# A selective-scan layer: how VectorE's fills are shared out between two steps, where GpSimd's input rows lie, and when the first copy of z is taken

## The chip, the cores and the metric

The kernel runs on one core of a Trainium2 chip. Its engines work side by side: TensorE (PE) for matmuls, VectorE (DVE), ScalarE (ACT) and GpSimd (POOL) for elementwise work, SyncE (SP) for issuing transfers. The metric is the device time of one execution in microseconds (us): the median of several runs. Lower is better.

## What is computed

The program is a chain of four layers on an image batch of shape (3, 256, 48, 48): a block with attention, two 3x3 convolutions, and a selective-scan (Mamba) layer, each behind a group norm and added to its input. The change touches the last layer alone. Cut to what matters, it is

```python
xz = einsum('blc,dc->bld', layernorm(x), in_proj_w)
x_in, z = split(xz, 2)                       # 512 channels each
u = silu(causal_conv1d(x_in, conv_w))        # 4 taps
dt_raw, B_ssm, C_ssm = split(u @ x_proj_w.T) # 16 states
dt = softplus(dt_raw @ dt_proj_w.T + dt_proj_b)
A = -exp(A_log)

def step(hst, inp):                          # over 2304 tokens
    dt_t, B_t, C_t, u_t = inp
    dA = exp(dt_t[:, :, None] * A)
    hst = hst * dA + dt_t[:, :, None] * B_t[:, None, :] * u_t[:, :, None]
    return hst, einsum('bdn,bn->bd', hst, C_t)

y = (scan(step) + u * D_param) * silu(z)
out = y @ out_proj_w.T
```

## The kernel before, in words

The 3 x 2304 tokens are cut into 18 chunks of 384 tokens (`todo`). The states of a chunk are 512 channels x 16 = 8192 rows, which are 64 tiles of 128 rows. They are worked through in 8 *steps* of 8 rows each: a step is `(at, m, h)`, with the chunk `at`, the block of 128 channels `m` (0 to 3) and the half `h` (0 or 1). So even steps have h = 0, odd ones h = 1, and the two steps of one `m` are a pair. The text counts the steps of a chunk from 0 to 7.

A step has one tile `hs` of the shape (128, 2, 4, 385): two groups `g` of B's rows by four quarters `q` of the channels, and per run one starting state and 384 tokens. There are three such buffers. The tile is filled with dt * u * B, then each of its eight runs is scanned in place, and the result is multiplied by C and summed. In detail, by the lines of the profile:

- `spread` (L1681) reads dt and dt * u from DRAM into the layout of the scan, with transfers that SyncE issues: `dtr` for all four quarters, `dtur` for quarters 2 and 3. `spread_pe` (L1689) puts dt * u for quarters 0 and 1 into the PSUM tile `ps_r` by matmuls. There is one `ps_r`, so a pair's matmuls wait until the pair before has read it.
- `fill` writes a step's products: VectorE quarters 0 and 1 of both groups, from `ps_r` (L1711, 1536 elements a partition), GpSimd quarters 2 and 3, from `dtur` (L1715, 1536 elements). Both read B's rows from SBUF. It stands at the end of the step before.
- `first_states` (L1724) and `last_states` (L1730) copy the one column of states that passes from chunk to chunk, on ScalarE.
- `decay` (L1740) makes exp(dt * A) for one run on ScalarE, in one of three PSUM tiles `ps_da`. It is issued three scans ahead, so that the decay of scan n + 3 waits until scan n has read the same tile.
- `scan` (L1748) runs the recurrence over one run on VectorE. The order of the eight runs is quarters 0, 1 of group 0, then of group 1, then quarters 2, 3 of group 0 and of group 1: the runs that VectorE filled come first.
- `times_c` (L1765) multiplies a step's states by C on GpSimd (3072 elements), behind the GpSimd fill of the next step. `add_states` (L1777, L1782) sums them over the states with matmuls, one step later. `gate` (L1789) multiplies by silu(z) on VectorE, at the end of an odd step, three steps later.

Beside the scan of one chunk the next chunk is prepared and the last one is projected and stored. These stages stand in the tables `plan`, `after` and `gating`: each has a slot 0 to 15 (a step is two slots of four scans), a place in the slot, and the chunk's offset. Places are `MID` (after the second scan and the decay issued with it), `DONE` (after the third), `LATE` (after the fourth), and `PE_` (matmuls, at the middle or the end of a step). A line in the table of this case:

```python
(14, MID, 1, lambda k: take_z(k, 0, 0)),
```

Slot 14 is the first half of step 7, and `take_z` (L1349) copies the first quarter of z from the PSUM bank 0 to SBUF on ScalarE. The bank was written by `project_z` (L1341), and `project_z` of the second quarter needs the same bank next. Ahead of this copy in the same place stands `inverse_root` (L1241, L1242). The two PSUM banks `bank[0]` and `bank[1]` serve all stages in turn, and each stage's matmuls wait until ScalarE or VectorE has read what was there: `taps` (L1264, the convolution) and `take_u` (L1273), `silu` (L1278, with table loads at L1278 and L228), `project_u` (L1284) and `take_dbc` (L1292), `project_dt` (L1310), `softplus` (L1319 to L1321), `take_dt` (L1326, L1327, on VectorE) and `keep_dt` (L1331), `project_y` (L1353, L1355) and `store` (L1365), `less_mean` (L1222), `centre` (L1235, L1237), `square_mean` (L1229), `normalise` (L1246, on VectorE), `tokens` (L1256).

The program's order on TensorE, VectorE, ScalarE and GpSimd is the order in which this code is written: `keep_order` ties each instruction behind the one before it on its engine. Instructions of different engines, and an instruction that needs the result of an earlier one on its own engine, wait on semaphores.

Of the kernel before, what the change touches and what calls it, by code (L numbers as in the profile page):

```python
# [9 lines left out]
F32 = mybir.dt.float32  # L10
I32 = mybir.dt.int32
AF = mybir.ActivationFunctionType
ALU = mybir.AluOpType
# [3 lines left out]
P = 128  # L17
# [8 lines left out]
CH = 384  # L26
# [57 lines left out]
def net(  # L84
# [21 lines left out]
    nc = tc.nc  # L106
# [273 lines left out]
    with ExitStack() as l0:  # L380
# [36 lines left out]
        with ExitStack() as p1:  # L417
# [15 lines left out]
            for b in ORDER:  # L433
# [3 lines left out]
                for ct in range(CT):  # L437
                    for j in range(parts):
                        at = slice(j * N // parts, (j + 1) * N // parts)
# [15 lines left out]
                bb = small.tile([P, 2], F32, name="bb")  # L455
# [592 lines left out]
        chunks = [(b, c) for b in ORDER for c in range(NCH)]  # L1048
# [58 lines left out]
    rooms, w3v, chunks, stored = {}, {}, {}, set()  # L1107

    def room(k, name):
        return rooms[name][k.at % len(rooms[name])]  # L1110
# [228 lines left out]
    def project_z(k, m, j):  # L1339
        for ct in range(CT):  # L1340
            nc.tensor.matmul(  # L1341
                bank[j], w("in", ct * 512 + m * P, P), k.xn[:, ct, DCONV - 1 :],
                start=ct == 0, stop=ct == CT - 1,
            )

    def take_z(k, m, j):
        if m == 0:
            k.sz = room(k, "sz")
        nc.scalar.copy(k.sz[:, m, :], bank[j])  # L1349
# [14 lines left out]
    def store(k, mo):  # L1364
# [7 lines left out]
    MID, DONE, LATE, PE_ = range(4)  # L1372
# [39 lines left out]

    gating = [
        (13, PE_, 1, lambda k: project_z(k, 0, 0)),
        (14, MID, 1, lambda k: take_z(k, 0, 0)),
        (14, PE_, 1, lambda k: project_z(k, 1, 0)),
        (15, MID, 1, lambda k: take_z(k, 1, 0)),
        (15, PE_, 1, lambda k: project_z(k, 2, 0)),
# [237 lines left out]
    with ExitStack() as l3:  # L1656
# [5 lines left out]
        scn = l3.enter_context(tc.tile_pool(name="scn", bufs=2, reuse_waits="tile"))  # L1662
# [10 lines left out]
        def spread(k, m):  # L1673

            dtr = scn.tile([P, 4, CH], F32, name="dtr")
            dtur = scn.tile([P, 2, CH], F32, name="dtur")
            for t, src in ((dtr, k.dtd), (dtur, k.dtud)):
                src = src[m & 2][:, m & 1, :]
                for i in range(4):
                    r = slice(32 * i, 32 * i + 32)  # L1680
                    nc.sync.dma_start(t[r], src.rearrange("(q d) n -> d q n", d=32))  # L1681
            return dtr, dtur
# [13 lines left out]
        steps = [(at, m, h) for at in range(len(todo)) for m in range(DI) for h in range(2)]  # L1696
        tiles = {}
# [4 lines left out]
        for t in slots:  # L1702
            nc.vector.memset(t[:, :1], 0.0)

        def fill(s):

            at, m, h = steps[s]
            k = chunks[at]
            hs = tiles[s]
            bb = k.bc[0][:, 2 * h : 2 * h + 2, :].unsqueeze(2).broadcast_to([P, 2, 2, CH])  # L1710
            nc.vector.tensor_tensor(  # L1711
                hs[:, :, 0:2, 1:],
                k.ps[:, :, :CH].unsqueeze(1).broadcast_to([P, 2, 2, CH]), bb, ALU.mult,
            )
            nc.gpsimd.tensor_tensor(  # L1715
                hs[:, :, 2:4, 1:],
                k.rows[m][1].unsqueeze(1).broadcast_to([P, 2, 2, CH]), bb, ALU.mult,
            )

        def first_states(s):  # L1720
            at, m, h = steps[s]
            src = zero if chunks[at].c == 0 else state[m, h]
            hs = tiles[s] = scn.tile([P, 2, 4, CH + 1], F32, name="hs", bufs=3)
            nc.scalar.copy(hs[:, :, :, 0], src.rearrange("p (g q) -> p g q", g=2))  # L1724

        def last_states(s):
            at, m, h = steps[s]
# [64 lines left out]
        last = len(todo) - 1  # L1792
        k = chunks[0]
        k.rows = {0: spread(k, 0)}
        spread_pe(k, 0)
        first_states(0)
        fill(0)
        for n in range(3):
            decay(n)
        for s, (at, m, h) in enumerate(steps):  # L1800
            if m == 0 and h == 1 and at + 2 <= last:
                fetch(at + 2)
            for part in range(8):
                j = 4 * m + 2 * h + part // 4
                scan(s, part)
                decay(8 * s + part + 3)
                if part == 0 and h == 0:
                    c, n = (at, m + 1) if m + 1 < DI else (at + 1, 0)
                    if c <= last:
                        rows = getattr(chunks[c], "rows", {})  # L1810
                        chunks[c].rows = {**rows, n: spread(chunks[c], n)}
                if part == 4 and s + 1 < len(steps):
                    first_states(s + 1)
                if part % 4 == 1:
                    run(at, j, MID)
                if part % 4 == 2:
                    run(at, j, DONE)
                if h == 1 and part == 7 and s >= 3:
                    gate(*steps[s - 3][:2])
                if part % 4 == 3:  # L1820
                    run(at, j, LATE)
                if part == 3:
                    run(at, j, PE_)
            if s + 1 < len(steps):
                fill(s + 1)
# [10 lines left out]
        k = chunks[last]  # L1836
# [37 lines left out]
def net_kernel(tc, *args):  # L1874

    with tc.tile_pool(name="flag", bufs=1) as pool:
        flag = pool.tile([1, 1], I32, name="flag")
        net(tc, *args, flag, False)
        bad = tc.nc.values_load(flag[:1, :1])
        with tc.If(bad > 0):  # L1880
            net(tc, *args, None, True)
# [77 lines left out]
```

## Time and profile before

| | |
|---|---|
| median of 5 runs | 3459.01 us (3453.64 to 3464.20) |
| the profiled execution | 3455.04 us, span 3453.7 us |
| scan layer within the span | first fill at 2020 us, last scan ends at 3432 us, end at 3454 us |
| one chunk of the scan layer (chunk 10) | 2811.93 to 2890.77 us |
| one scan (L1748) | 0.94 us, 0.85 us from start to start |
| VectorE fill (L1711) | 1.74 us |
| GpSimd fill (L1715), product with C (L1765) | 3.45 us, 6.19 us |
| one decay (L1740) | 0.58 us |
| granted TensorE clock, mean of the span | 0.944 |

The span reaches from the first to the last instruction of the profiled execution; its time as the runs measure it is 1.3 us longer. A row of the timeline gives start, duration, engine, line, operation, tile written and tiles read, and in brackets how long the engine was idle before and who ended that. A row of a group adds the count, the busy time, the mean duration in ns, and the idle time before. A row of a stretch gives for PE, PE's weight loads, DVE, ACT and POOL the busy time and the count, then the granted clock, the share of the DMA engines and GB/s. Rows of waits give the waiting engine and line, who was waited for, the total, the times and the longest.

### The profile page before, as it was taken

To read this page: it belongs to the slowest core of one execution; us is meant where nothing else is said; L and a number is where in the kernel's file an instruction comes from. 1 tells how busy PE (TensorE), PEld (TensorE's weight loads), DVE (VectorE), ACT (ScalarE), POOL (GpSimd) and SP (SyncE) were. 2 spreads that over 40 slices of the span, in tenths; PEclk is the share of its full clock that TensorE was granted. 3 is DMA by queue.
4 is the path that set the end of the run, shared out by engine and by line. 5 is a ranking of instruction groups with operands and counts; after the bars stand their busy time and mean duration, and the time that the engine had idled before them with its cause. 6 is when DMAs were issued, how large, how long until landed. Compare 5 with 4: busy or idle time off the path is not lost.

```text
span 3453.7 us, 51943 instructions
## 1 busy us (share of the span) xinstructions
PE 3121.8 (90%) x20170; PEld 1500.1 (43%) x20170; DVE 2939.8 (85%) x3234; ACT 2351.6 (68%) x3508; POOL 1430.5 (41%) x385
## 2 busy tenths in 40 slices
PE   7999999999999999879999988888888888888885
PEld 4334343443433335457777743333344433333331
DVE  4798899859899994589965379999999999999997
ACT  3788888758888884422224457777777777777774
POOL 0000000000000001110000059999999999999997
PEclk9999999999999999999999989889999999988997
DMA  4000000010000003756301134444444444544441
GB/s 187 5 10 8 8 10 8 8 42 7 9 6 8 10 8 112 248 187 215 133 29 60 52 91 115 109 106 114 120 102 114 103 111 110 120 113 110 113 111 43
DMA packets 167603, 273.95 MB, mean 79 GB/s; under 512 B 30049, under 2 KB 134561, under 8 KB 165426
## 3 DMA queue, kind: packets, MB, share of 16 engines
q1 hardware_dynamic: 154114, 250.48, 26.9%
q10 hardware_dynamic: 13232, 20.06, 1.8%
q8 instruction: 160, 2.62, 0.3%
q14 instruction: 97, 0.79, 0.1%
HBM read 223.12 MB, written 47.10 MB: 78 GB/s over the span
## 4 chain that ended last, share of the span: by engine, by line
PE 53%; DVE 33%; ACT 8%; DMA 3%; issue 2%; POOL 0%; SPq 0%; DVEq 0%; ACTq 0%; POOLq 0%
DVE hs L1748 21%; PE ps_s L637 16%; PE acc L650 14%; PE ps_c L1513 8%; DVE hs L1711 4%; PE ps_g L1222 2%; ACT ps_da L1740 2%; DVE u L295 2%; PE ps_y L461 2%; PE ps_m L664 1%; PE ps_s L1030 1%; PE ps_m L710 1%; ACT L1278 1%; ACT L228 1%; PE acc L528 1%
## 5 line engine op out<-in xcount | busy, mean ns | idle before, releaser
L1748 DVE TENSOR_TENSOR_SCAN hs<-ps_da,hs 128x385 f32<-128x385 f32 x1152 | 1005.5, 938 | 54.3 <-ACT ps_da L1740 35.5
L641 ACT ACTIVATE pt<-ps_s 128x1024 f32<-128x1024 f32 x972 | 942.3, 1022 | 154.8 <-PE ps_s L637 142.4
L856 DVE TENSOR_TENSOR part<-part,pt 128x2048 f32<-128x2048 f32 x396 | 906.6, 2289 | 41.3 <-ACT pt L641 18.5
L1740 ACT ACTIVATE ps_da<-dtr,u 128x384 f32<-128x384 f32 x1152 | 655.9, 582 | 270.7 <-DVE hs L1748 247.9
L163 POOL TENSOR_TENSOR rstd<-ve,mhalf 128x2 f32<-128x2 f32 (+1 forms) x26 | 16.3, 629 | 1475.1 <-DVE ve L161 1475.1
L637 PE MATMUL ps_s<-q,kt 32*128 32x512 f32 (+1 forms) x4320 | 576.7, 592 | 0.1
L650 PE MATMUL acc<-pt,vt 128*32 128x512 f32 (+1 forms) x4320 | 521.1, 561 | 0.2
L1765 POOL TENSOR_TENSOR hc<-hs,x 128x3072 f32<-128x3072 f32 x72 | 445.9, 6193 | 21.1 <-DVE hs L1748 19.2
L1513 PE MATMUL ps_c<-vt,u 128*128 128x288 f32 x1728 | 433.6, 412 | 20.9 <-DVE u L262 20.9
L1765 POOL TENSOR_TENSOR hc<-hs,bc 128x3072 f32<-128x3072 f32 x71 | 438.9, 6181 | 17.3 <-DVE hs L1748 16.2
L1264 PE MATMUL ps_g<-u 128*128 128x384 f32 x1152 | 387.7, 492 | 8.2 <-ACT sz L1349 3.5
L1513 PEld LDWEIGHTS ps_c<-vt,u 128*128 128x128 f32 x1728 | 331.9, 193 | 117.2 <-issue 19.2
L1264 PEld LDWEIGHTS ps_g<-u 128*128 128x128 f32 x1152 | 214.6, 190 | 180.3 <-ACT ps_da L1740 18.7
L637 PEld LDWEIGHTS ps_s<-q,kt 32*128 32x128 f32 x4320 | 195.6, 183 | 198.8 <-issue 120.0
L1782 PE MATMUL ps_y<-hc,u 128*32 128x384 f32 x2304 | 245.6, 549 | 13.2 <-POOL hc L1765 13.2
L1715 POOL TENSOR_TENSOR hs<-dtur,x 128x1536 f32<-128x1536 f32 x72 | 248.1, 3446 | 6.6 <-DMA dtur<-dtud 6.6
L1715 POOL TENSOR_TENSOR hs<-dtur,bc 128x1536 f32<-128x1536 f32 x72 | 249.5, 3465 | 0.0
L650 PEld LDWEIGHTS acc<-pt,vt 128*32 128x32 f32 x4320 | 94.7, 108 | 353.1 <-issue 326.5
L1310 PE MATMUL ps_g<-wconv,u 17*128 17x384 f32 x144 | 79.2, 684 | 82.8 <-ACT x L1331 82.8
L1782 PEld LDWEIGHTS ps_y<-hc,u 128*32 128x32 f32 x2304 | 64.5, 117 | 172.1 <-issue 153.1
L321 POOL MEMSET xpad<- 128x212 f32 x12 | 5.6, 469 | 314.2 <-ACT xpad L1564 235.6
L1222 PE MATMUL ps_g<-wconv,u 128*128 128x384 f32 x144 | 82.9, 747 | 52.0 <-ACT x L1331 52.0
(246 smaller groups left out, 3615.6 us busy)
## 6 DMA issues: line engine op xcount, KB each, us to landing
wconv<-in_we SPq DMA_DIRECT2D x144, 384.0 KB, 4.3
dtr<-dtd SPq DMA_DIRECT2D x288, 192.0 KB, 3.9
dtur<-dtud SPq DMA_DIRECT2D x288, 96.0 KB, 4.2
wconv<-xd SPq DMA_DIRECT2D x36, 384.0 KB, 4.3
x<-bcd SPq DMA_DIRECT2D x72, 192.0 KB, 6.1
dtd<-x SPq DMA_DIRECT2D x36, 384.0 KB, 2.8
bc<-bcd SPq DMA_DIRECT2D x72, 192.0 KB, 6.0
yc<-ycat ACTq DMA_DIRECT2D x18, 576.0 KB, 4.8
```

The source lines that it names most:

```text
L637: nc.tensor.matmul(s[:, j, cols], kt[r, mt * P : (mt + 1) * P], q[r, :n], start=True, stop=True,)
L641: nc.scalar.activation(p[:, h0 : h0 + 2, :], s, AF.Exp)
L650: nc.tensor.matmul(acc[h * HD : (h + 1) * HD, :n], vt[:, mt, g * P + h * HD : g * P + (h + 1) * HD], p[:, h, cols], start=mt == 0, stop=mt ...
L856: ): nc.vector.tensor_tensor(part, first, p, ALU.add)
L1222: nc.tensor.matmul(bank[to], w3v["less"][:, int(to != ct), :], k.xg[:, ct, :], start=ct == 0, stop=ct == CT - 1,)
L1264: nc.tensor.matmul(bank[m % 2], w3v["wtap"][:, tap, ct, m * P : (m + 1) * P], k.xn[:, ct, tap : tap + CH], start=tap == 0 and ct == 0, sto ...
L1513: nc.tensor.matmul(pc[:, :HN], u[:, i, dy, ct, m * P : (m + 1) * P], vt[:, i, ct, dy * TW : dy * TW + HN], start=ct == 0 and dy == 0, stop ...
L1715: nc.gpsimd.tensor_tensor(hs[:, :, 2:4, 1:], k.rows[m][1].unsqueeze(1).broadcast_to([P, 2, 2, CH]), bb, ALU.mult,)
L1740: nc.scalar.activation(slots[n % 3][:, 1 : CH + 1], chunks[at].rows[m][0][:, q, :], AF.Exp, scale=amat[:, col : col + 1],)
L1748: nc.vector.tensor_tensor_scan(b, slots[(8 * s + part) % 3][:, : CH + 1], b, 0.0, ALU.mult, ALU.add)
L1765: nc.gpsimd.tensor_tensor(hc, tiles[s][:, :, :, 1:], cb.broadcast_to([P, 2, 4, CH]), ALU.mult)
L1782: nc.tensor.matmul(k.y_ps[32 * q : 32 * q + 32, :CH], fold, hc[:, g, q, :], start=False, stop=h == 1 and g == 1,)
```

## The change

Three things change.

- VectorE's fill of a pair is cut differently. Before, an even and an odd step's four runs each (two groups of two quarters) were filled ahead of the step. Now six runs are filled ahead of the even step: its own four, and the two of group 0 of the odd step. The two that remain, of group 1, are filled ahead of the odd step. The tile of the odd step is therefore taken one step earlier. GpSimd's fill stays as it is.
- `dtur` gets rows of 400 elements instead of 384, of which elements 8 to 391 are used: the rows start 32 bytes behind the start of the tile, and the tile of two rows grows by 128 bytes, as do the places of the tiles behind it.
- `take_z` of the first quarter moves from `MID` to `DONE` in slot 14, one scan and one decay later.

```diff
-        (14, MID, 1, lambda k: take_z(k, 0, 0)),
+        (14, DONE, 1, lambda k: take_z(k, 0, 0)),
...
-            dtur = scn.tile([P, 2, CH], F32, name="dtur")
+            dtur = scn.tile([P, 2, 16 + CH], F32, name="dtur")[:, :, 8 : 8 + CH]
...
+        def states(s):
+
+            if s not in tiles:
+                tiles[s] = scn.tile([P, 2, 4, CH + 1], F32, name="hs", bufs=3)
+            return tiles[s]
+
+        def b_rows(s, lo, hi):
+            at, m, h = steps[s]
+            rows = chunks[at].bc[0][:, 2 * h + lo : 2 * h + hi, :]
+            return rows.unsqueeze(2).broadcast_to([P, hi - lo, 2, CH])
+
+        def fill_upper(s, lo, hi):
+
+            k = chunks[steps[s][0]]
+            nc.vector.tensor_tensor(
+                states(s)[:, lo:hi, 0:2, 1:],
+                k.ps[:, :, :CH].unsqueeze(1).broadcast_to([P, hi - lo, 2, CH]),
+                b_rows(s, lo, hi), ALU.mult,
+            )
+
         def fill(s):
 
             at, m, h = steps[s]
-            k = chunks[at]
-            hs = tiles[s]
-            bb = k.bc[0][:, 2 * h : 2 * h + 2, :].unsqueeze(2).broadcast_to([P, 2, 2, CH])
-            nc.vector.tensor_tensor(
-                hs[:, :, 0:2, 1:],
-                k.ps[:, :, :CH].unsqueeze(1).broadcast_to([P, 2, 2, CH]), bb, ALU.mult,
-            )
+            if h == 0:
+                fill_upper(s, 0, 2)
+                fill_upper(s + 1, 0, 1)
+            else:
+                fill_upper(s, 1, 2)
             nc.gpsimd.tensor_tensor(
-                hs[:, :, 2:4, 1:],
-                k.rows[m][1].unsqueeze(1).broadcast_to([P, 2, 2, CH]), bb, ALU.mult,
+                states(s)[:, :, 2:4, 1:],
+                chunks[at].rows[m][1].unsqueeze(1).broadcast_to([P, 2, 2, CH]),
+                b_rows(s, 0, 2), ALU.mult,
             )
 
         def first_states(s):
             at, m, h = steps[s]
             src = zero if chunks[at].c == 0 else state[m, h]
-            hs = tiles[s] = scn.tile([P, 2, 4, CH + 1], F32, name="hs", bufs=3)
-            nc.scalar.copy(hs[:, :, :, 0], src.rearrange("p (g q) -> p g q", g=2))
+            nc.scalar.copy(states(s)[:, :, :, 0], src.rearrange("p (g q) -> p g q", g=2))
```

## The prediction

> **What bounds the kernel now.** The change lives in the scan layer, the last 1430 us, so the page's shares over the whole span say little. I read the stage first, over one chunk in steady state (chunk 10, 2812 to 2891 us; a chunk is 8 steps of 8 scans). The columns are the busy time of each engine:
>
> ```profile
> 2812.00:2891.00 79.00, 67.32 (x282) 31.14 (x281) 75.79 (x86) 61.67 (x121) 76.57 (x18) 0.89 0.46 111
> ```
>
> VectorE (third) and GpSimd (fifth) are both full to 96%, and TensorE (first) to 85%. Who waits for whom decides, so next come VectorE's waits from 2040 to 3430 us, and GpSimd's groups:
>
> ```profile
> DVE hs L1748 <- ACT ps_da L1740: 34.9, 52, 1.5
> DVE hs L1748 <- DVE hs L1711: 0.5, 1, 0.5
> DVE ps_g L1326 <- ACT x L1321: 0.2, 1, 0.2
> ...
> L1765 POOL TENSOR_TENSOR hc<-hs,x 128x3072 f32<-128x3072 f32 x72 | 445.9, 6193 | 21.1 <-DVE hs L1748 19.2 <-DVE x L1789 1.7 <-POOL hs L1715 0.3
> L1715 POOL TENSOR_TENSOR hs<-dtur,bc 128x1536 f32<-128x1536 f32 x72 | 249.5, 3465 | 0.0
> L1715 POOL TENSOR_TENSOR hs<-dtur,x 128x1536 f32<-128x1536 f32 x72 | 248.1, 3446 | 6.6 <-DMA dtur<-dtud 6.6
> L1040 POOL TENSOR_TENSOR x<-x,xc 128x768 f32<-128x768 f32 x18 | 34.5, 1917 | 109.3 <-ACT x L1035 91.2 <-DMA wconv<-in_we 18.0
> ```
>
> VectorE never waits for GpSimd here, only for ScalarE's decays; GpSimd waits for VectorE. So VectorE carries the stage, and GpSimd follows close behind. The timeline of VectorE in chunk 10 (start, length, line, idle before) shows where the waits stand and how the fills sit between the scans:
>
> ```profile
> 2811.85 0.53 DVE L1789 TENSOR_TENSOR sz<-ps_y,sz 128x384 f32<-128x384 f32 x1
> 2812.30 1.75 DVE L1711 TENSOR_TENSOR hs<-ps_r,x 128x1536 f32<-128x1536 f32 x1
> 2814.15 6.91 DVE L1748 TENSOR_TENSOR_SCAN hs<-ps_da,hs 128x385 f32<-128x385 f32 x8
> 2820.97 1.73 DVE L1711 TENSOR_TENSOR hs<-ps_r,x 128x1536 f32<-128x1536 f32 x1
> 2822.81 6.91 DVE L1748 TENSOR_TENSOR_SCAN hs<-ps_da,hs 128x385 f32<-128x385 f32 x8
> ...
> 2835.17 4.36 DVE L1748 TENSOR_TENSOR_SCAN hs<-ps_da,hs 128x385 f32<-128x385 f32 x5 [0.58 <-ACT ps_da L1740]
> ...
> 2853.64 4.36 DVE L1748 TENSOR_TENSOR_SCAN hs<-ps_da,hs 128x385 f32<-128x385 f32 x5 [0.57 <-ACT ps_da L1740]
> ...
> 2887.25 0.96 DVE L1748 TENSOR_TENSOR_SCAN hs<-ps_da,hs 128x385 f32<-128x385 f32 x1 [1.10 <-ACT ps_da L1740]
> 2888.12 0.93 DVE L1246 TENSOR_TENSOR wconv<-wconv,ps_g 128x768 f32<-128x768 f32 x1
> 2888.97 1.80 DVE L1748 TENSOR_TENSOR_SCAN hs<-ps_da,hs 128x385 f32<-128x385 f32 x2
> ```
>
> The waits stand in three places: at the fourth scan of steps 2 and 4, behind a SiLU and its two table loads, and at the sixth of step 7, behind the inverse root and the first copy of z. Last, TensorE, which no VectorE wait names, and which is the point of this forecast:
>
> ```profile
> 2817.04 10.59 PE L1264 MATMUL ps_g<-u 128*128 128x384 f32 x32 [0.42 <-ACT x L1349]
> 2827.56 1.50 PE L1782 MATMUL ps_y<-hc,u 128*32 128x384 f32 x16
> 2828.99 0.92 PE L1689 MATMUL ps_r<-x,u 32*128 32x384 f32 x4
> ...
> 2847.28 0.91 PE L1689 MATMUL ps_r<-x,u 32*128 32x384 f32 x4
> ```
>
> From 2817.04 to 2848.19 it runs with no idle. It starts on ScalarE's copy of z (L1349), which is queued behind a decay that waits for the second scan of step 0. Its two L1689 rows write the ps_r that the fills of steps 2 and 4 read: they end at 2829.91 and 2848.19, and those fills start at 2830.08 and 2848.56. The slack is 0.17 and 0.37 us.
>
> **The change, part by part.**
>
> *The fills on VectorE.* A pair of steps has fills of 1536 and 1536 elements; now 1536 and 768, then 768. Dependent work starts 1.85 us after the start of a full fill (2812.30 to 2814.15), 1.84 in odd steps. Independent work starts 0.08 before its predecessor ends (2811.85 against 2811.93), so a 768 behind the full fill starts after 1.67. The nearest row of 768 elements is L1246: the next instruction starts 0.85 after it. I take this, since it also has one operand in PSUM and one in SBUF. The first scan of an even step needs the full fill alone, and of an odd step neither, so neither waits for the 768 to drain. Even: 1.67 + 0.85 - 1.85 = **+0.67**. Odd: 0.85 - 1.84 = **-0.99**. A line through L1789 (384 elements, next start 0.45 later) and the full fill (1.67) gives 0.86 as well. Bounds: 0.83 (half of 1.67) and 0.85 + 0.19 = 1.04, if the even scan waits for the 768 as a scan waits for its fill now (0.10 of gap, 0.08 of lost overlap).
>
> [...]
>
> *The wait that is added.* The 768 fill ahead of an even step writes the odd step's states, in the buffer that L1765 reads two steps before. It is queued ahead of the even step's scans, so if L1765 is late all of them are. In chunk 10 that L1765 ends 3.3 us or more before its place (for step 4: 2840.74 + 6.22 = 2846.96 against 2850.2), so it costs nothing while GpSimd trails by no more than 3 us beyond today.
>
> *The walk through chunk 10* (shift of each step's end against before; a wait that goes is worth its idle plus 0.11, as step 2 is 9.81 long and step 0, without one, 9.12):
> - Step 0: +0.67. The copy of z sits behind the second scan, so TensorE's run moves by +0.67 as well.
> - Step 1: -0.99, leaving -0.32.
> - Fill of step 2: VectorE could start it 0.32 early, but ps_r now ends at 2829.91 + 0.67; with 0.05 for the hand-over it starts at 2830.63, +0.55. This is a new wait of about 0.87.
> - Step 2: +0.55 + 0.67 - 0.69 (the wait behind the SiLU is covered now) = +0.53.
> - Step 3: -0.99 in VectorE's own work, but its last scan waits for a decay behind the store's copy, which waits for TensorE's projection of the same run (+0.67): the step ends at +0.36.
> - Fill of step 4: 2848.19 + 0.67 + 0.05 = 2848.91, +0.35; step 4 ends at +0.35 + 0.67 - 0.68 = +0.34.
> - Step 5: -0.99 would bring the softplus product (L1326) to 2.49 after the step's start, but ScalarE's softplus ends 3.16 after it; L1326 moves from 3.48 to 3.20: -0.28, leaving +0.06.
> - Step 6: +0.67, nothing to cover it: +0.73.
> - Step 7: ScalarE's chain (centre, TensorE's mean of squares, inverse root) is fixed to the end of step 6, so the -0.99 is lost to it.
>
> *The copy of z a part later* helps here: the sixth scan's decay no longer stands behind the copy (0.48, and 0.23 waiting for TensorE), and the scan starts 6.55 instead of 7.21 after step 7's start: -0.66, leaving **+0.07 a chunk**. What is late next is the copy itself, by one decay: the projection queued behind it on TensorE starts after other matmuls anyway. Bounds: 0 (the wait only moves to the next decay) and -0.71 (copy and wait both gone).
>
> *GpSimd's rows 32 bytes off.* GpSimd has 76.6 of 79 us of work and VectorE does not wait for it, so a faster fill buys nothing in the steady state. Bounds by its rows per element: 3.10 us (rate of L1765, 2.02 ns) and 3.83 (rate of L1040, 2.50 ns), against 3.45 now. The two L1715 rows read different buffers of B and differ by 0.02; that is nearest, so I take no change. The padding leaves the four DMAs' count and pieces alone, and no VectorE wait names them.
>
> *Ends.* In the first chunk TensorE has 5 us of slack at both fills, so about -2 us; in the last, which prepares no next chunk, GpSimd trails by up to 4.5 us, so -0.4 at most.
>
> **Sum:** 16 x 0.07 - 2 - 0.4 = -1.3 us on the profiled execution's 3455.0 us (span 3453.7), that is 3453.7. This run lies 4.0 below the median of 3459.0, so on the median: **3458 us**.
>
> **The rivals.**
> - *Faster: TensorE's run is not the limit* (it starts earlier, or has idle that the trace hides). Then the steps add to 0.67 - 0.99 - 0.02 - 0.99 - 0.02 - 0.28 + 0.67 - 0.66 = -1.62 a chunk: 16 x 1.62 + 2 = -28, 3431 us. For it: VectorE's own work does shrink, by 0.32 a pair. Against: 31 us without an idle mark. A half-way case, with only some of the 0.67 passed on, gives 3438 to 3450.
> - *Slower: the even scan waits for the second fill.* At 1.04 for a 768 fill, steps 0, 4 and 6 each cost 0.19 more: 0.57 x 17 = +10, 3468 us. It decides from about 1.01 on, where the total passes 7 us. Against: the scan needs only the first fill.
> - *Slower: GpSimd's fill slows down.* A chunk lasts 78.3 to 78.9 us in this trace, against 76.5 of GpSimd's work: 0.23 to 0.30 a fill to spare. At 3.83 (+0.38) it is short by 0.08 to 0.15, x 8 x 17 = +11 to +20: about 3473 us. It decides from about 3.75 on. For it: GpSimd is nearly full. Against: the two rows 0.02 apart.
> - *The change does nothing:* the offset alone may be that, and it is inside the forecast.
>
> [...]
>
> **How the numbers follow.** About 0.2% (7 us) is what a measurement of this kernel can tell from no change. Forecast (3452 to 3464 of its own): 0.52. TensorE not the limit: 0.13, half-way 0.10. Second fill waited for: 0.12. GpSimd slower: 0.10. Something slower that I don't see: 0.03. So faster 0.23, same 0.52, slower 0.25. The range 3438 to 3474 leaves out the full first rival and tails of the others.
>
> **What would show it.** In the profile after: fills of 1.75 and 0.93 us; scans directly behind the odd one; no ScalarE wait at the fourth scan of steps 2 and 4; a smaller one at the sixth of step 7; and a new one, VectorE's fill waiting for TensorE's L1689, about 0.9 us in each step 2. If that last is missing and TensorE has idle between its two L1689 rows, I am wrong on the fast side; a GpSimd fill of over 3.75 us, or a gap between the second fill and the scan, puts me wrong on the slow side.

## The result, and the profile after

The changed kernel takes 3454.24 us (median of 25 runs, 3449.55 to 3463.25), the kernel before, run beside it, 3457.09 us (median of 47 runs). The ratio is 0.9993, 95% interval [0.9988, 0.9999]: within the 0.2% that a measurement of this kernel can tell from no change, as forecast, and just below 1.

The same views as before. First VectorE's waits from 2040 to 3430 us in the changed kernel (engine and line that wait, who was waited for, total us, times, longest):

```profile
DVE hs L1766 <- ACT ps_da L1758: 27.1, 37, 0.9
DVE ps_g L1326 <- ACT x L1321: 11.3, 17, 1.2
DVE hs L1719 <- PE ps_r L1689: 4.3, 16, 0.3
DVE x L1807 <- PE ps_y L1800: 3.4, 8, 0.5
DVE sz L1807 <- PE ps_y L1800: 3.2, 8, 0.4
DVE hs L1766 <- POOL hs L1733: 1.6, 2, 0.9
DVE hs L1719 <- POOL hc L1783: 0.5, 1, 0.5
```

The scans (now L1766) wait 27.1 us for decays instead of 34.9. New are the softplus wait (L1326), 11.3 instead of 0.2 us, and two waits on TensorE in step 2: the gate (L1807), 6.6 us in all, and the fill (L1719), 4.3 us. The three waits for GpSimd, 2.1 us together, all stand in the last chunk. Next, the timeline of VectorE in chunk 10 of the changed kernel: steps 0 to 2, the last scan of step 3, the middle of step 5, and the sixth scan of step 7.

```profile
2812.04 0.53 DVE L1807 TENSOR_TENSOR sz<-ps_y,sz 128x384 f32<-128x384 f32 x1
2812.49 2.61 DVE L1719 TENSOR_TENSOR hs<-ps_r,x 128x1536 f32<-128x1536 f32 x2
2815.02 6.89 DVE L1766 TENSOR_TENSOR_SCAN hs<-ps_da,hs 128x385 f32<-128x385 f32 x8
2821.84 0.93 DVE L1719 TENSOR_TENSOR hs<-ps_r,x 128x768 f32<-128x768 f32 x1
2822.69 6.89 DVE L1766 TENSOR_TENSOR_SCAN hs<-ps_da,hs 128x385 f32<-128x385 f32 x8
2829.98 0.56 DVE L1807 TENSOR_TENSOR sz<-ps_y,sz 128x384 f32<-128x384 f32 x1 [0.40 <-PE ps_y L1800]
2830.80 2.62 DVE L1719 TENSOR_TENSOR hs<-ps_r,x 128x1536 f32<-128x1536 f32 x2 [0.27 <-PE ps_r L1689]
...
2847.81 0.96 DVE L1766 TENSOR_TENSOR_SCAN hs<-ps_da,hs 128x385 f32<-128x385 f32 x1 [0.76 <-ACT ps_da L1758]
...
2861.77 0.57 DVE L1326 SCALAR_TENSOR_TENSOR ps_g<-ps_g,x 128x384 f32<-128x384 f32 x1 [0.63 <-ACT x L1321]
...
2887.03 0.96 DVE L1766 TENSOR_TENSOR_SCAN hs<-ps_da,hs 128x385 f32<-128x385 f32 x1 [0.82 <-ACT ps_da L1758]
```

Two fills ahead of an even step take 2.53 us from the start of the first to the start of the scan (2812.49 to 2815.02), where one took 1.85; the fill of 768 ahead of an odd step takes 0.85 (2821.84 to 2822.69). So an even step is 0.68 longer and an odd one 0.99 shorter in VectorE's own work. The fourth scan of steps 2 and 4 no longer waits. TensorE's run in the same chunk:

```profile
2817.89 10.59 PE L1264 MATMUL ps_g<-u 128*128 128x384 f32 x32 [0.37 <-ACT x L1349]
2828.41 1.50 PE L1800 MATMUL ps_y<-hc,u 128*32 128x384 f32 x16
2829.84 0.91 PE L1689 MATMUL ps_r<-x,u 32*128 32x384 f32 x4
...
2848.13 0.91 PE L1689 MATMUL ps_r<-x,u 32*128 32x384 f32 x4
```

It starts 5.77 us after step 0 does (2812.12), as against 5.11 before, and runs on without a gap; the gate waits for its L1800 (done at 2829.91) and the fill for its L1689 (done at 2830.75). GpSimd's fills are as they were (3452 and 3454 ns, before 3446 and 3465), so its rows 32 bytes off did nothing; one of the two groups:

```profile
L1733 POOL TENSOR_TENSOR hs<-dtur,x 128x1536 f32<-128x1536 f32 x72 | 248.5, 3452 | 6.7 <-DMA dtur<-dtud 6.7
```

The walk through chunk 10, step end by step end, in us after the end of the chunk before:

| | step 0 | 1 | 2 | 3 | 4 | 5 | 6 | 7 |
|---|---|---|---|---|---|---|---|---|
| before | 9.12 | 17.79 | 27.60 | 36.26 | 46.07 | 56.86 | 68.11 | 78.84 |
| after | 9.79 | 17.46 | 28.12 | 36.65 | 46.45 | 56.99 | 68.91 | 78.43 |
| shift measured | +0.67 | -0.33 | +0.52 | +0.39 | +0.38 | +0.13 | +0.80 | -0.41 |
| shift forecast | +0.67 | -0.32 | +0.53 | +0.36 | +0.34 | +0.06 | +0.73 | +0.07 |

Seven of eight fit within 0.07. The eighth doesn't, and it is the one that makes the time. In the kernel before, step 7 has two lengths: its chunks last 78.1 to 78.3 us or 78.7 to 79.1, mixed, and chunk 10 is one of the long ones. Against a short one the changed chunk is 0.10 longer. The experiments turned to what makes this length.

### The profile page after: what moved, and what is told of

Same layout as the page of the kernel before. It is cut to its first block, busy times and chain, and to the rows that moved or that the text cites. A ratio compares the mean times of both kernels' runs of the same rounds, so it can differ in the third digit from the quotient of the medians.

```text
span 3453.7 us, 51999 instructions
## 1 busy us (share of the span) xinstructions
PE 3117.4 (90%) x20170; PEld 1498.2 (43%) x20170; DVE 2936.8 (85%) x3306; ACT 2353.2 (68%) x3508; POOL 1430.6 (41%) x385
## 5 line engine op out<-in xcount | busy, mean ns | idle before, releaser
L1766 DVE TENSOR_TENSOR_SCAN hs<-ps_da,hs 128x385 f32<-128x385 f32 x1152 | 1003.5, 935 | 30.5 <-ACT ps_da L1758 27.1
L1800 PE MATMUL ps_y<-hc,u 128*32 128x384 f32 x2304 | 245.1, 548 | 19.5 <-POOL hc L1783 19.1
L1733 POOL TENSOR_TENSOR hs<-dtur,x 128x1536 f32<-128x1536 f32 x72 | 248.5, 3452 | 6.7 <-DMA dtur<-dtud 6.7
L1733 POOL TENSOR_TENSOR hs<-dtur,bc 128x1536 f32<-128x1536 f32 x72 | 248.7, 3454 | 0.0
L1310 PE MATMUL ps_g<-wconv,u 17*128 17x384 f32 x144 | 79.2, 684 | 85.0 <-ACT x L1331 85.0
L1800 PEld LDWEIGHTS ps_y<-hc,u 128*32 128x32 f32 x2304 | 64.2, 117 | 177.9 <-issue 141.0
L1222 PE MATMUL ps_g<-wconv,u 128*128 128x384 f32 x144 | 80.3, 725 | 62.1 <-ACT x L1331 62.1
```

The source lines that it names most:

```text
L1222: nc.tensor.matmul(bank[to], w3v["less"][:, int(to != ct), :], k.xg[:, ct, :], start=ct == 0, stop=ct == CT - 1,)
L1733: nc.gpsimd.tensor_tensor(states(s)[:, :, 2:4, 1:], chunks[at].rows[m][1].unsqueeze(1).broadcast_to([P, 2, 2, CH]), b_rows(s, 0, 2), ALU.mult,
L1766: nc.vector.tensor_tensor_scan(b, slots[(8 * s + part) % 3][:, : CH + 1], b, 0.0, ALU.mult, ALU.add)
L1800: nc.tensor.matmul(k.y_ps[32 * q : 32 * q + 32, :CH], fold, hc[:, g, q, :], start=False, stop=h == 1 and g == 1,)
```

## The experiments

All ratios are to the kernel before, run beside it on the same chip; lengths of steps and chunks come from one profiled execution each.

### One part at a time

**The new fills alone** (the offset and the place of the copy of z as before):

```diff
-        (14, DONE, 1, lambda k: take_z(k, 0, 0)),
+        (14, MID, 1, lambda k: take_z(k, 0, 0)),
...
-            dtur = scn.tile([P, 2, 16 + CH], F32, name="dtur")[:, :, 8 : 8 + CH]
+            dtur = scn.tile([P, 2, CH], F32, name="dtur")
```

> The new fills alone, with the copy of z and the rows of dt*u as before. Theory (TensorE's run from the copy of z to the ps_r matmuls, and ScalarE's chains, hold the steps, so that VectorE's shorter work buys nothing): step 7 keeps its wait of about 0.9 us at the sixth scan, so a chunk is 0.6 to 0.75 us longer than before, 16 of them +10 to +12, first and last chunk -2.4 together: about +8 us, ratio 1.0015 to 1.003. Rival (the fills alone carry the change, VectorE's own work counts, -0.32 a pair and the waits behind the SiLU gone): 1 us or more less a chunk, ratio 0.995 or below.

3470.86 us, ratio 1.0035 [1.0023, 1.0047]. The fills alone lose, as expected, and more than the 1.0015 to 1.003 forecast. Steps 0 to 6 are those of the changed kernel within 0.01 us; step 7 is 10.71 instead of 9.59 (means over chunks 4 to 15).

**The copy of z later, alone** (on the kernel before):

```diff
-        (14, MID, 1, lambda k: take_z(k, 0, 0)),
+        (14, DONE, 1, lambda k: take_z(k, 0, 0)),
```

> The copy of z a part later alone. Theory: the sixth scan of step 7 starts about 0.66 us earlier in each of 16 chunks, TensorE's run starts up to 0.2 later against step 0 and that fits into the slack of its ps_r matmuls: -9 to -11 us, ratio about 0.997. Rival (the copy's wait only moves to the next decay or to TensorE): ratio 0.999 to 1.001.

3456.19 us, ratio 0.9995 [0.9986, 1.0004]: the gain did not come. The decay of the sixth scan did pass ahead of the copy, but step 7 is 10.44 us long with it and without it (means over chunks 4 to 15). What took the gain is on TensorE. The eight matmuls of L1222 (less_mean), for which step 7's normalisation waits, in chunk 10 of the kernel before and then of this one:

```profile
2876.87 5.05 PE L1222 MATMUL ps_g<-wconv,u 128*128 128x384 f32 x8 [3.21 <-ACT x L1331]
```

```profile
2875.99 5.42 PE L1222 MATMUL ps_g<-wconv,u 128*128 128x384 f32 x8 [3.21 <-ACT x L1331]
```

The same eight matmuls last 4.54 to 5.28 us in chunks 1 to 15 of the kernel before, and 5.42 to 5.49 in those of this one. That is the granted clock, which comes below, with the account of what the later copy is worth.

**The rows 32 bytes off, alone**:

```diff
-            dtur = scn.tile([P, 2, CH], F32, name="dtur")
+            dtur = scn.tile([P, 2, 16 + CH], F32, name="dtur")[:, :, 8 : 8 + CH]
```

> The rows of dt*u 32 bytes off alone. Theory: GpSimd's fill stays at 3.45 us within 0.02, ratio 1.000 within 0.001. Rival (the offset changes GpSimd's rate): its fill moves by 0.1 us or more, and even then a faster fill leaves the time as it is, while a slower one by over 0.25 us lengthens each chunk.

3457.08 us, ratio 0.9997 [0.9988, 1.0005]: nothing, as expected.

**The odd step's fill ahead in the middle four steps only** (steps 2 to 5), where a wait used to cover it, with the later copy and the offset:

```diff
-            if h == 0:
-                fill_upper(s, 0, 2)
+            ahead = m in (1, 2)
+            fill_upper(s, int(ahead and h == 1), 2)
+            if ahead and h == 0:
                 fill_upper(s + 1, 0, 1)
-            else:
-                fill_upper(s, 1, 2)
```

> The changed kernel, but the odd step's fill is taken ahead for the two middle pairs alone (steps 2 and 3, steps 4 and 5), where it covers ScalarE's SiLU; the first and the last pair are filled as before. Theory: TensorE's run is not pushed back (no +0.67 in step 0), step 6 loses nothing, steps 3 and 5 gain about 0.3 us each and step 7 0.66: a chunk is 1.1 to 1.3 us shorter than before, in all -18 to -21 us, ratio 0.994 to 0.995. Rival (more of the pairs cut is better, since each saves 0.32 us on VectorE): slower than the whole change, ratio to before above 0.9993.

3443.22 us, ratio 0.9957 [0.9944, 0.997]: it beats both kernels. The waits on TensorE are gone: apart from two single ones of 0.6 and 0.5 us, for GpSimd and ScalarE, these are VectorE's waits from 2040 to 3430 us in this kernel:

```profile
DVE hs L1765 <- ACT ps_da L1757: 21.6, 29, 0.8
DVE ps_g L1326 <- ACT x L1321: 11.3, 17, 1.2
```

Yet the mean of chunks 1 to 16 is 77.89 us (before 78.44), not the 1.1 to 1.3 less that was expected. (Over these 16 chunks that is 8.8 us; the first chunk gives 3.0 more and the last 0.9.) L1222 lasts 5.36 to 5.49 us in eleven of the chunks 1 to 15 and 4.27 to 4.54 in the other four, and these four last 77.1 to 77.3 us: the expected length comes only where the clock is better.

### The clock

The granted clock of TensorE in the scan layer is 1.00 or 0.50, nothing between (clock records of the kernel before and the changed one). The stretches here are cut where it changes, over steps 5 to 7 of chunk 10 of the changed kernel (busy time and count of PE, PE's loads, DVE, ACT, POOL; then the granted clock, DMA share, GB/s):

```profile
2861.08:2864.49 3.41, 0.00 (x0) 0.00 (x0) 2.71 (x6) 1.74 (x4) 3.41 (x1) 1.00 1.08 212
2864.49:2867.91 3.42, 1.97 (x3) 1.16 (x4) 3.42 (x5) 2.95 (x7) 3.42 (x2) 0.50 1.08 227
...
2871.32:2874.73 3.41, 2.66 (x16) 0.47 (x15) 3.38 (x5) 2.49 (x6) 3.41 (x1) 0.50 0.00 0
2874.73:2878.15 3.42, 0.29 (x1) 0.29 (x2) 3.39 (x6) 2.25 (x6) 3.42 (x2) 1.00 0.00 0
2878.15:2881.56 3.41, 3.41 (x6) 1.67 (x6) 3.41 (x5) 2.81 (x7) 1.75 (x2) 0.50 0.77 223
```

All stretches are multiples of 3.413 us, on one grid: from 2020 to 3440 us the clock changes 68 times in the kernel before, over 412 windows of 3.4133 us, and 60 times in the changed one, over 411, each time within 0.001 us of the grid. After the two windows here in which TensorE worked 0.00 and 0.29 us the next is at half clock. The half clock here begins behind TensorE's long pause in step 5, where project_dt (L1310) waits for ScalarE (L1331), and it slows L1222 in steps 6 and 7. The eight matmuls in this chunk, of which 3.41 us lie in the window at half clock from 2878.15 us on (at full clock all the time they take 2.85 us, as a kernel below shows, and half of 3.41 more is 4.55):

```profile
2877.86 4.54 PE L1222 MATMUL ps_g<-wconv,u 128*128 128x384 f32 x8 [3.88 <-ACT x L1331]
```

A window ahead of half clock need not be quite idle, as the 0.29 us here and the rows of the cut kernel below show (1.11 us of work).

How long L1222 takes sets the length of step 7. In all the kernels of this table it starts 3.16 to 3.17 us ahead of the end of step 6, and this is what follows in chunks 1 to 15 (us; the means are over chunks 4 to 15):

| kernel | L1222 | mean | step 7 | step 7 less L1222, in each chunk |
|---|---|---|---|---|
| before | 4.54 to 5.28 | 4.76 | 10.22 to 10.96 | 5.68 |
| rows off, alone | 4.54 to 5.26 | 4.72 | 10.22 to 10.94 | 5.68 |
| new fills alone | 4.29 to 5.49 | 5.03 | 9.97 to 11.18 | 5.68 |
| copy of z later, alone | 5.42 to 5.49 | 5.46 | 10.40 to 10.47 | 4.98 |
| after | 4.54 to 4.86 | 4.61 | 9.52 to 9.84 | 4.98 |

The last column is the same within 0.01 in every chunk. So the later copy is worth 0.70 us in step 7 wherever it stands, and all else that step 7 gains or loses is L1222's length. The later copy alone lost its 0.70 to an L1222 that is 0.70 longer on average.

Since the grid didn't move with the kernel's work (one grid over the whole scan layer in each of the two executions above), a chunk can settle into step with it. 23 windows are 78.507 us, and this is what the mean chunk is (end of chunk 3 to end of chunk 15, over 12) in kernels that should differ:

| kernel | mean chunk, us | in windows |
|---|---|---|
| before | 78.507 | 23.00 |
| after | 78.507 | 23.00 |
| copy of z later, alone | 78.521 | 23.00 |
| rows off, alone | 78.482 | 22.99 |
| extra matmuls on before / on the later copy / on after | 78.550 / 78.503 / 78.499 | 23.01 / 23.00 / 23.00 |
| after, a tap left out | 78.505 | 23.00 |
| new fills alone | 79.625 | 23.33 |
| before, a tap left out | 80.212 | 23.50 |
| an extra product of 96 elements | 85.324 | 25.00 |
| an extra product of 384 elements | 85.061 | 24.92 |
| middle steps only | 77.924 | 22.83 |
| extra matmuls on middle steps only | 78.652 | 23.04 |

The kernels that have not been told of yet follow below. In the row with 24.92, one chunk lasts 81.97 us and the others 85.3 to 85.4. With the new fills alone three chunks repeat (79.1, 80.1, 79.7 us: 70 windows), on before with a tap left out two (79.5 and 81.0: 47 windows).

The two kernels with an extra product show how a chunk is pulled to such a length, since one starts below 25 windows (85.333 us) and the other above. Chunk by chunk, with the time of L1222 in it:

| | chunk 1 | 2 | 3 | 4 | 5 |
|---|---|---|---|---|---|
| 96 elements: chunk | 84.82 | 85.11 | 85.18 | 85.28 | 85.29 |
| L1222 | 4.85 | 5.07 | 5.22 | 5.27 | 5.31 |
| 384 elements: chunk | 85.77 | 85.64 | 85.46 | 85.42 | 85.36 |
| L1222 | 5.49 | 5.32 | 5.19 | 5.11 | 5.09 |

After a chunk that is too short, the grid stands later against the work of the next one, more of L1222 lies at half clock, and the chunk gets longer. After one that is too long it is the other way round.

### Extra matmuls against the half clock

If the pauses make the half clock, work in them should keep the clock up. The matmuls of L1689 are repeated, with the same values into the same place:

```diff
-            t = psr.tile([P, 2, 512], F32, name="ps_r")
-            for q in range(2):
+            k.ps = psr.tile([P, 2, 512], F32, name="ps_r")
+            rows_pe(k, m, 6 if m == 3 else 1)
+
+        def rows_pe(k, m, times):
+            for q in list(range(2)) * times:
...
             if s >= 1:
                 add_states(s - 1)
+            if m == 2 and h == 1:
+                rows_pe(chunks[at], 3, 3)
```

On the kernel before:

> The kernel before, with TensorE kept at work where it idles for 4.9 us in step 5 and 3.2 us in step 6: the two matmuls of L1689 for step 6 are written six times instead of once in step 5, and three times more in step 6 (the same values into the same place). Theory (the granted clock of 0.5 over steps 5 to 7 makes the eight matmuls of L1222 last 4.5 to 5.5 us, and step 7's sixth scan waits behind them): the clock stays at 1.0, L1222's run takes 2.7 to 2.8 us, its two copies (L1235) don't wait, and the end of the inverse root moves from 5.98 us after step 7's start to about 4.8. The sixth scan's wait (0.88 us a chunk on average) goes: step 7 falls from 10.36 to about 9.5 us, a chunk from 78.44 to about 77.55, and the time by some 14 us: 3442 to 3446, ratio 0.995 to 0.9965. Rival (the clock doesn't answer to these idle stretches, or ScalarE's own work sets step 7): within 0.1%, and L1222's run stays at 4.5 to 5.5 us.

On the later copy of z alone:

> The copy of z later alone (as in the second run), with the same extra matmuls. Theory (the gain of the later copy was given back because L1222 fell wholly into the stretch of half clock, 5.49 us instead of 4.5 to 5.0): L1222 takes 2.7 to 2.8 us, step 7 falls from 10.41 to about 9.5 us, a chunk from 78.42 to about 77.5, the time to 3441 to 3445, ratio 0.995 to 0.9965; the same as the kernel before with these matmuls, because at full clock the inverse root ends early enough with or without the later copy. Rival (the later copy gains nothing for another reason, such as ScalarE's work in step 7): ratio 0.999 to 1.0, step 7 at 10.4.

On the version with the middle steps only:

> The change with the odd step's fill ahead in the middle four steps only (the fourth run, ratio 0.9957), with the same extra matmuls. Theory: step 7 falls from 10.11 to about 9.5 us, a chunk from 77.89 to about 77.3, the time to some 3433 to 3436, ratio 0.9925 to 0.994. Rival: 0.9957 as without them.

On the changed kernel:

> The changed kernel with the same extra matmuls. Theory: L1222 takes 2.7 to 2.8 us instead of 4.5 to 4.9, the inverse root ends 0.6 to 0.7 us earlier in step 7, and of the sixth scan's wait (0.83 us) some 0.15 is left: step 7 falls from 9.50 to about 8.85 us, a chunk from 78.41 to about 77.75, the time to 3442 to 3445 (ratio to the kernel before 0.995 to 0.9965). Rival (the change is limited by TensorE's run in steps 0 to 4 alone, and what step 7 gains is lost there): a chunk stays at 78.4, ratio 0.999 to 1.0.

Ratios: 1.0001 [0.9992, 1.001], 0.9999 [0.999, 1.0008], 0.999 [0.9981, 0.9999] and 0.9992 [0.9983, 1.0001]. None of the four gains that were forecast came. Yet L1222 became faster in most chunks of the kernel before; this is chunk 10 of it, with the repeated rows (L1692) in the pauses:

```profile
2866.82 4.14 PE L1692 MATMUL ps_r<-x,u 32*128 32x384 f32 x24 [0.33 <-DVE hs L1713]
2872.65 1.55 PE L1310 MATMUL ps_g<-wconv,u 17*128 17x384 f32 x4 [1.69 <-ACT x L1331]
...
2880.61 2.45 PE L1692 MATMUL ps_r<-x,u 32*128 32x384 f32 x12
2883.90 2.85 PE L1222 MATMUL ps_g<-wconv,u 128*128 128x384 f32 x8 [0.83 <-ACT x L1331]
```

With L1222 at 2.85 us (granted clock 1.00 from 2884 to 2888 us) most chunks of it last 77.86 us, 0.65 below 23 windows. But then the half clock falls on a later place in each following chunk's work, until it begins a window earlier, covers L1222 again, and one chunk takes 79.5 to 79.8 (once 79.05, with half clock behind L1222 instead). Mostly two short chunks and a long one make some 69 windows, and the mean is where it was. The half clock became rarer (14% of chunks 1 to 16 instead of 20%) but did not go. The repeated matmuls did not hold the clock as other work did. In the kernel before and the changed one, from 2100 to 3355 us, each window at full clock with 1.97 us or more of work was followed by full clock, and each with 0.95 or less by half clock; none lay between. Here a window with 2.70 us, all of it theirs, is followed by half clock:

```profile
3103.03:3106.44 3.41, 2.70 (x18) 1.47 (x14) 3.34 (x7) 1.08 (x4) 3.41 (x1) 1.00 1.12 226
3106.44:3109.86 3.42, 2.44 (x4) 1.16 (x4) 3.42 (x5) 3.09 (x8) 3.42 (x2) 0.50 1.06 254
```

No run tells why.

In the middle version VectorE's fills now wait for TensorE's rows (L1692), 6.5 us in 14 waits, and step 2 is 10.46 us long instead of 9.87.

One thing is clean in these runs: chunks whose L1222 and step 7 lie at full clock throughout can be compared. They last 77.86 us on the kernel before (one of them 77.65) and 77.94 on the changed one, +0.08; the later copy alone gives 77.63 to 77.64 in three such chunks. L1222 at full clock is not enough: in other chunks of the later copy it takes 2.85 us, but half clock lies behind it, and they last 78.4 to 78.8.

### Is TensorE's run the limit?

The convolution's fourth tap is left out in the scan layer, so that TensorE's run is shorter.

```diff
-                    start=tap == 0 and ct == 0, stop=tap == DCONV - 1 and ct == CT - 1,
+                    start=tap == 0 and ct == 0, stop=tap == hi - 1 and ct == CT - 1,
...
-        (0, PE_, 1, lambda k: taps(k, 0, 0, 4)),
-        (1, PE_, 1, lambda k: taps(k, 1, 0, 4)),
+        (0, PE_, 1, lambda k: taps(k, 0, 0, 3)),
+        (1, PE_, 1, lambda k: taps(k, 1, 0, 3)),
...
-        (3, PE_, 1, lambda k: taps(k, 2, 0, 4)),
-        (4, PE_, 1, lambda k: taps(k, 3, 0, 4)),
+        (3, PE_, 1, lambda k: taps(k, 2, 0, 3)),
+        (4, PE_, 1, lambda k: taps(k, 3, 0, 3)),
```

On the changed kernel:

> The changed kernel, but the convolution's fourth tap is left out in the scan layer (6 instead of 8 matmul pairs in each of the four groups of L1264, with one fourth of that work gone). TensorE's run from the copy of z to the two L1689 rows is 2.7 us shorter at the first and 5.4 at the second. Theory (the odd step's gain is lost to TensorE's run): the new waits on TensorE vanish, the gate's and the fill's in step 2, and the walk gives -0.3 us at the end of step 1, -1.3 after step 4, -1.6 after step 7. Step 2 falls from 10.67 to about 9.8 us, step 3 from 8.53 to 7.7, step 5 stays at 10.5. A chunk would last 76.8 to 77.5 (the longer figure if the half clock covers all of L1222 in step 7, as it did in the fourth run): 3428 to 3440, ratio 0.992 to 0.9955. Rival (GpSimd or ScalarE holds the chunk, not TensorE): no step before 5 gets shorter by more than 0.2 us, and the ratio stays above 0.9985.

Ratio 0.9992 [0.9983, 1.0001]. The steps came out, the chunk didn't. VectorE in chunk 10: no wait at step 2's gate and fill, none in step 3, and a longer one for the softplus in step 5 than the 0.63 of the changed kernel.

```profile
2827.78 0.53 DVE L1807 TENSOR_TENSOR sz<-ps_y,sz 128x384 f32<-128x384 f32 x1
2828.23 2.61 DVE L1719 TENSOR_TENSOR hs<-ps_r,x 128x1536 f32<-128x1536 f32 x2
...
2838.44 6.90 DVE L1766 TENSOR_TENSOR_SCAN hs<-ps_da,hs 128x385 f32<-128x385 f32 x8
...
2859.19 0.57 DVE L1326 SCALAR_TENSOR_TENSOR ps_g<-ps_g,x 128x384 f32<-128x384 f32 x1 [1.36 <-ACT x L1321]
```

Step ends of chunk 10 against the kernel before are +0.67, -0.33, -0.34, -1.33, -1.22 for steps 0 to 4, close to the -0.3 and -1.3 expected. Then they are -0.74, -0.07 and -0.34. TensorE, now with time to spare, pauses in step 4, and the pause costs it the clock just where the next matmuls (L1284, project_u) are wanted; the waits in its timeline and the stretches around them:

```profile
2848.81 4.38 PE L1284 MATMUL ps_g<-u 128*96 128x384 f32 x8 [2.47 <-ACT u L1278]
...
2875.28 5.49 PE L1222 MATMUL ps_g<-wconv,u 128*128 128x384 f32 x8 [4.32 <-ACT x L1331]
```

```profile
2846.51:2849.92 3.41, 1.11 (x4) 0.64 (x5) 3.41 (x4) 3.38 (x3) 3.41 (x2) 1.00 1.01 206
2849.92:2853.34 3.42, 3.42 (x7) 1.67 (x6) 3.42 (x5) 2.83 (x8) 3.42 (x1) 0.50 0.17 58
2853.34:2856.75 3.41, 3.41 (x22) 1.08 (x20) 3.40 (x5) 3.03 (x7) 3.41 (x2) 1.00 0.06 14
```

The window after the one with 1.11 us of work is at half clock, and L1284 takes 4.38 us instead of 2.75. It starts 1.8 us earlier in the chunk than in the changed kernel (38.4 instead of 40.2 us from its start) and ends only 0.15 earlier; project_dt starts at 44.9 in both, and the softplus ends 0.9 earlier where VectorE comes 1.6 earlier. L1222 lies at half clock for all but 0.13 of its 5.49 us. In the chunks before, the window that hits L1284 stands 78.507 us earlier each time:

```profile
2614.40:2617.81 3.41, 3.41 (x7) 1.69 (x6) 3.41 (x5) 2.81 (x8) 3.41 (x1) 0.50 0.21 69
2692.91:2696.32 3.41, 3.41 (x7) 1.68 (x6) 3.41 (x5) 2.82 (x8) 3.41 (x1) 0.50 0.16 58
```

From chunk 4 to 15 each chunk lasts 78.49 to 78.51 us. So TensorE's run does hold steps 2 and 3 of the changed kernel, as the prediction has it. But taking the hold away gave 1.6 us by the end of step 4 (-1.22 instead of +0.38), and none of it was left over the chunks.

On the kernel before:

> The kernel before, with the same tap left out. Theory (before, TensorE's two rows end 0.17 and 0.37 us ahead of need, so VectorE does not wait for them): steps 0 to 5 keep their lengths within 0.1 us (step 3 may lose up to 0.1), a chunk lasts 78.3 to 78.5, ratio 0.9985 to 1.0005. Rival (TensorE's run sets the pace before as well, by a hand-over that the profile gives to other causes): steps 2 and 4 are over 0.3 us shorter and the ratio is under 0.997.

3482.12 us, ratio 1.0076 [1.0063, 1.0089]: less work, and slower. Steps 0 to 3 keep their lengths, as expected, so TensorE is not the limit there in the kernel before. But TensorE now pauses in step 4 ahead of L1284, where the kernel before has no gap, and in every other chunk L1284 takes about twice the 2.82 us of before (5.44 in chunk 10 below; 4.3 to 4.4 in the chunks between):

```profile
2871.25 5.44 PE L1284 MATMUL ps_g<-u 128*96 128x384 f32 x8 [3.47 <-ACT u L1278]
```

Step 4 is 10.46 us on average instead of 9.79, step 5 11.21 instead of 10.79, and step 7 11.04 instead of 10.44.

### One more instruction on VectorE

A small product in step 6 should show whether a chunk grows by what is put into it. (The first of the two kernels; the second has 384 elements.)

```diff
+        pad = wp.tile([P, CH], F32, name="pad")
...
                 scan(s, part)
+                if m == 3 and h == 0 and part == 1:
+                    u = chunks[at].u[:, 3, :96]
+                    nc.vector.tensor_tensor(pad[:, :96], u, u, ALU.mult)
```

> The kernel before, with one more VectorE instruction in step 6 of each chunk: a product of 96 elements that nothing reads, some 0.14 us by the line through the rows of 384 and 1536 elements. Step 6 has no wait that could cover it and step 7 is timed from its end. Theory (a chunk is tied to the clock: the half clock begins at one of two window limits in step 5, a chunk is 78.33 or 78.8 us long accordingly, and the mix settles at 23 windows of 3.413 us = 78.507): step 6 grows by 0.14, but the mix shifts to the shorter kind, with step 7 shorter on average; the mean chunk stays between 78.40 and 78.52. Ratio 0.9995 to 1.0005. Rival (steps add up): every chunk grows by 0.14 us, the mean to 78.58; ratio 1.0005 to 1.001.

> The same with 384 elements, some 0.45 us. Theory: both kinds of chunk would then be over 78.507 us (78.78 and 79.25), so the balance is lost; the half clock drifts earlier against the chunk until it takes another pattern, as in the first run (three windows, a gap, two more, with L1222 at 5.5 us). The mean chunk is 78.95 to 79.2 us, more than the instruction itself: ratio 1.0025 to 1.0037. Rival (steps add up): 78.89, ratio 1.0021, with step 7 as long as before.

Ratios 1.0336 [1.0323, 1.035] and 1.0327 [1.0314, 1.0341]: far outside both expectations. VectorE in chunk 10 with 96 elements, then GpSimd in the same kernel:

```profile
2936.31 6.29 DVE L1809 TENSOR_TENSOR pad<-x 128x96 f32<-128x96 f32 x1
```

```profile
2932.93 6.17 POOL L1765 TENSOR_TENSOR hc<-hs,x 128x3072 f32<-128x3072 f32 x1
2939.07 3.41 POOL L1715 TENSOR_TENSOR hs<-dtur,x 128x1536 f32<-128x1536 f32 x1
```

The product ends at 2942.60, 0.12 us after GpSimd's fill: it lasted through the rest of one instruction of GpSimd and all of the next. So it is in most chunks. With 384 elements it ends 0.41 us after an instruction of GpSimd in all 18 chunks; in three of them that was the first one, and it took 3.13 to 3.21 us, and the chunk of 81.97 us is one of these. Why is not shown: it has two operands in SBUF, and the scan layer's other products on VectorE have one in PSUM and were short (0.53 to 0.56 us for each L1789 in the kernel before), but no run has the extra product with an operand in PSUM. The experiment therefore did not put in 0.14 and 0.45 us, and says nothing on the question as it was asked. By accident it still answers: in chunks 8 to 15 step 6 is 17.75 us long with 384 elements and 17.48 with 96 (means without chunk 11, which is 0.2 longer in both), and step 7 is 10.72 and 11.00. The chunks are equal, 85.33 us, 25 windows. What one step gained, the other gave back.

## Why the prediction was right, and what in it was not

It forecast 3458 us on the earlier median of 3459.0, 1.3 us less than before; the runs beside each other give 2.9 us less by the medians. The range held, and so did the likeliest case.

- *The fills.* +0.67 and -0.99 forecast; +0.68 and -0.99 measured. That the even scan waits for the second fill is refuted: of the 2.53 the first fill takes 1.67, so the second hands over after 0.86, not 1.04.
- *The walk to the end of step 6.* All seven shifts within 0.07. The new wait of 0.87 in step 2 is there: the fill starts 0.53 later in the chunk, where VectorE alone would bring it 0.32 earlier. But it stands in two parts (0.40 and 0.27 of idle time, the rest lost overlap): the gate ahead of the fill waits for add_states in the same run, and the fill waits less for it. The prediction did not name the gate.
- *TensorE's run as the limit.* Shown at steps 0 to 4 by the cut kernel. The first rival, "TensorE's run is not the limit", had its premise made true there, and its 3431 us did not come: 0.9992 of the kernel before. The step from shifts to time was wrong in the rival as well.
- *Step 7 and "leaving +0.07 a chunk".* This is the term that does not stand as written. Its parts are right: the later copy, forecast at -0.66, is worth -0.70, and with L1222 at 4.54 us in both kernels a chunk is 0.10 longer after the change (78.43 against 78.33). With step 7 at full clock it is 0.08. What the sum takes as given is how long L1222 lasts. In chunk 10, from which it is added up, that is 5.05 us before and 4.54 after, and these 0.51 are the whole way from +0.10 to the -0.41 in the last column of the walk. Over chunks 4 to 15 L1222 is 0.14 shorter on average, steps 0 to 6 are 0.85 longer and the copy gives 0.70: the mean difference is 0.00, and both settle at 23 windows. The row that should have warned was on show: a granted clock of 0.89 in the chunk.
- *Luck.* That the forecast was so close is in part luck. The later copy alone has a sum of -0.70 a chunk by the same account, and its mean chunk came back to 78.521 as well; the fills alone have some +0.8 and went to 79.625. The pull to 23 windows hides an error of the sum as it hides a gain.
- *GpSimd's rows.* No change, shown alone and in the groups; the rival of a slower GpSimd is refuted by 3452 and 3454 ns.
- *Ends.* -2 for the first chunk: 84.51 to 81.75 us in the two executions, though the second fill has a wait there that was not foreseen, as the odd step's states lie where `vt` was and that is still being stored:

```profile
2023.42 1.76 DVE L1719 TENSOR_TENSOR hs<-ps_r,x 128x1536 f32<-128x1536 f32 x1
2027.59 0.96 DVE L1719 TENSOR_TENSOR hs<-ps_r,x 128x768 f32<-128x768 f32 x1 [2.42 <-DMA xd<-vt]
...
2033.05 3.51 DVE L1766 TENSOR_TENSOR_SCAN hs<-ps_da,hs 128x385 f32<-128x385 f32 x4 [1.09 <-POOL hs L1733]
```

The fifth scan's wait for GpSimd (1.09, before 3.63) covers most of it. -0.4 for the last chunk was wrong: 72.08 to 72.25, as VectorE now waits there for GpSimd three times. The first chunk's gain is about what the measured ratio amounts to (0.07% is 2.4 us).

What stays open: that the chunk is drawn to whole numbers of windows was read from the traces, and no run set the clock from outside. Which kernels settle at 23.00 and which at 23.33 or 23.50 is not explained, and no kernel here ran the scan layer without half clock.

## What to carry to other kernels

Before adding up shifts of steps in a loop, look at the granted clock by windows of 3.4 us over one period of the loop: if the period is a whole number of windows, a small gain or loss may be given back, as here, and a single part's effect can't be read from the total. Then compare iterations in which the matmuls on the path take the same time, and look for changes that move the period off that number, as the version with the middle steps did (22.83 windows, 0.9957). Shortening an engine's work can lose time when its pauses grow with it (1.0076 for the cut on the kernel before).

## What the runs showed of the hardware

- Loops settled at 23.00, 23.33, 23.50 and 25.00 windows of 3.413 us, on three chips and with different work in them. Leaving out a quarter of a convolution's matmuls in the kernel before cost 0.76%.
- Half clock followed windows in which TensorE had worked 0.00, 0.29 and 1.11 of 3.41 us, and not only idle ones. In the kernel before and the changed one full clock followed each window at full clock with 1.97 us or more of work, but half clock also followed 2.70 us of the repeated matmuls.
- A VectorE product of 96 elements with both operands in SBUF lasted 6.29 us beside GpSimd. In chunk 10 it ended 0.12 us after GpSimd's fill, which stood at once behind the product with C that was running when it began. No run shows why.
